# Weighted sums of an attention layer as two float32r matmuls a unit, with the row sums from ones beside v

## The chip, the core and the metric

The kernel runs on one NeuronCore of a Trainium2 chip. The metric is the device time of one execution in microseconds. A core has five engines that work side by side[...]: TensorE (PE in the profile; PEld is its loading of weights), VectorE (DVE), ScalarE (ACT), GpSimd (POOL) and SyncE (SP), which here issues the transfers. Each engine executes its own queue in order.

## What is computed

Two attention layers follow each other on an input of 8 images, 512 channels, 32 x 32 pixels, so T = 1024 positions. Layer 0 is the one that the change touches. Cut to what matters:

```python
# layer 0, per image; 8 heads of 64 channels
h = group_norm(x, gn_w, gn_b)
q, k, v = split(qkv_w @ h + qkv_b)            # per head 64 x T
q, k, v = fake_quant(q), fake_quant(k), fake_quant(v)   # 8 bits, one range over the whole batch
w = softmax((q * scale).T @ (k * scale))      # T x T for each head
a = v @ w.T                                   # 64 x T
x = x + proj_w @ a + proj_b
# layer 1, per image; one head of 512 channels
x = x + wp @ attention(group_norm(x)) + bp
```

The range of fake_quant is that of all images, so no attention of layer 0 can start before the projections of all eight images are done.

## The kernel before

Phase 1 computes q, k and v of all images (`qkps` and `vps`), writes them to device memory and keeps their extremes; then it folds layer 1's weights (`fold`, `fold_b`). Phase 2 does layer 0's attention, its projection (`pj`) and all of layer 1.

The attention of layer 0 runs over units. A unit is one image b, one pair of heads j, one half hf of the 1024 queries and one tile s of 128 keys: 8 x 4 x 2 x 8 = 512 units. The eight units of one (b, j, hf) form a group; there are 64. For each unit `scores` makes two bf16 matmuls of 64 rows, one for each head, into the PSUM tile `st` (128 x 1024, two buffers), and ScalarE takes the exponential into `pt` in SBUF (four buffers). There is no maximum to subtract. VectorE adds the `pt` of a group into `acc`. `weighted` multiplies `pt` by the quantized v in fp32, one 64-column matmul for each head, and accumulates both heads in the two halves of one PSUM bank `av` (two buffers, so that a new group can start while the old bank is read). `finish`, called in the second iteration of the following group, gets the row sums from `acc` with two matmuls by ones (`sm`), copies them to SBUF (`rs`), takes their reciprocal on VectorE and multiplies `av` by it and by the scale of v into `ao`. It also writes one row for each head to `chk0`, from which the end of the kernel decides whether a general path has to redo the work.

The order on TensorE is written out by hand: `mm` ties each matmul to the one before it. `attention` is a generator that issues two units an iteration, in this order:

```python
scores(u + 2)
scores(u + 3)
weighted(u)
weighted(u + 1)
```

The generator `others` issues the projection and layer 1 of the images whose attention is done, in chunks of four fp32 matmuls of 128 x 128 x 512 (`pj`, `g`, `v2ps`, `s`, `o`). A chunk advances a counter by 4.0, an attention iteration advances `pos`, and the loop at the end keeps both in the ratio A_IMAGE / F_IMAGE, so that one image of attention lies beside one image of the other work. Image 0's attention has nothing to lie beside, since the other work needs its result first. In the group norm of layer 1 (`norm_steps`, matmuls `gps`) the other work yields gaps (GN_GAPS 8, 3 and 3), which only attention fills. The tiles of the other work use two PSUM banks (`bank`). Before the loop, `load_pair` fetches q, k and v of the next head pair and quantizes them with two VectorE operations each.

## Time and profile before

| | us |
|---|---|
| median of 3 runs | 3141.29 (3141.09 to 3143.08) |
| the profiled execution | 3143.79 |
| its span | 3142.1 |
| TensorE busy in it | 3058.7 (97%) |
| VectorE busy | 1676.8 (53%) |
| ScalarE busy | 706.2 (22%) |
| first scores of image 0 to its first `pj` | 757.26 to 867.10 |
| start of the last `pj` alone | 2929.53 |

The span is the profiled stretch of one execution. Busy times are of the engines' own instructions; overlapping ones count once in the sum, but their mean length is that of each, so a sum and a mean times a count can differ. A line number is that of the source; L351 is the helper `mm`, so that matmuls there are told apart by their tile names. In a group, the time after the second bar is how long the engine stood idle just before these instructions, and the names after it are what ended that idle time. One fp32 matmul leaves two records. A few per cent of the matmul records can be missing.

### The profile page before, as it was taken

How to read it: one execution, taken by the hardware profiler on the slowest of the kernel's cores; microseconds unless marked ns; L12 is line 12 of the kernel's file. 1: busy time of each engine (PE TensorE's matmuls, PEld its weight loads, DVE VectorE, ACT ScalarE, POOL GpSimd, SP SyncE). 2: the span in 40 equal slices, each digit the busy share in tenths (PEclk: the TensorE clock that was granted, in tenths of full speed). 3: DMA queues.
4: the chain of work that ended last, by engine and by line, in shares of the span. 5: the costliest groups of instructions: out<-in, count | busy, mean ns of one | idle time of the engine just before them, and what ended most of it. 6: DMA issues, size and time to landing. Idle time of an engine off the chain costs nothing.

```text
span 3142.1 us, 22609 instructions
## 1 busy us (share of the span) xinstructions
PE 3058.7 (97%) x8808; PEld 1192.6 (38%) x8808; DVE 1676.8 (53%) x1992; ACT 706.2 (22%) x793; POOL 20.3 (1%) x26
## 2 busy tenths in 40 slices
PE   8999999998899999999999999999999999999998
PEld 4444444444233333333333333333333333333343
DVE  5555544443983555546555645573555546554422
ACT  0000000003632322232223323232322332223001
POOL 0000000000000000000000000000000000000000
PEclk9999999998999999999999999999999999999999
DMA  6222221222110110011010101110110011000000
GB/s 251 101 107 101 100 80 74 80 89 89 61 41 20 47 47 20 23 45 47 21 41 27 61 20 48 43 32 20 48 47 21 27 41 47 21 21 4 14 11 18
DMA packets 90278, 161.55 MB, mean 51 GB/s; under 512 B 11056, under 2 KB 43824, under 8 KB 89520
## 3 DMA queue, kind: packets, MB, share of 16 engines
q1 hardware_dynamic: 88576, 151.32, 13.8%
q10 hardware_dynamic: 1584, 8.68, 0.7%
q8 instruction: 71, 1.16, 0.2%
q14 instruction: 47, 0.39, 0.0%
HBM read 92.56 MB, written 67.11 MB: 51 GB/s over the span
## 4 chain that ended last, share of the span: by engine, by line
PE 90%; DVE 6%; issue 2%; DMA 1%; ACT 0%; POOL 0%; DVEq 0%; ACTq 0%
PE o L351 15%; PE s L351 15%; PE qkps L243 14%; PE av L351 11%; PE g L351 7%; PE v2ps L351 7%; PE vps L262 7%; PE pj L351 7%; PE st L351 3%; DVE acc L407 3%; PE sm L351 2%; DVE rs L429 2%; PE fold L280 1%; PE fold_b L294 1%; DVE acc L405 1%
## 5 line engine op out<-in xcount | busy, mean ns | idle before, releaser
L402 ACT ACTIVATE pt<-st,esc 128x1024 f32<-128x1024 f32 x512 | 544.0, 1112 | 735.8 <-PE st L351 709.1
L351 PE MATMUL av<-pt,v 128*64 128x512 f32 x2048 | 507.6, 617 | 0.0
L407 DVE TENSOR_TENSOR acc<-acc,pt 128x1024 f32<-128x1024 f32 x384 | 467.9, 1220 | 55.0 <-ACT pt L402 43.9
L351 PE MATMUL o<-p,v 128*128 128x512 f32 x1024 | 466.5, 602 | 2.3 <-ACT rs L559 1.4
L351 PE MATMUL s<-g,h 128*128 128x512 f32 x1024 | 465.2, 602 | 0.0
L243 PE MATMUL qkps<-h,wqkv 128*128 128x512 f32 x1024 | 445.4, 596 | 2.6 <-DVE h L115 2.6
L351 PEld LDWEIGHTS o<-p,v 128*128 128x128 f32 x1024 | 186.4, 190 | 275.5 <-issue 233.2
L351 PEld LDWEIGHTS s<-g,h 128*128 128x128 f32 x1024 | 187.1, 190 | 269.7 <-issue 230.0
L243 PEld LDWEIGHTS qkps<-h,wqkv 128*128 128x128 f32 x1024 | 194.3, 191 | 241.7 <-issue 237.2
L429 DVE RECIPROCAL rs<-rs 128x512 f32<-128x512 f32 x64 | 214.6, 3354 | 82.0 <-ACT rs L428 82.0
L351 PE MATMUL g<-h,wa 128*128 128x512 f32 x512 | 236.7, 615 | 6.1 <-DVE h L115 6.1
L351 PE MATMUL pj<-ao,wp 128*128 128x512 f32 x512 | 233.9, 604 | 0.0
L351 PEld LDWEIGHTS av<-pt,v 128*64 128x64 f32 x2048 | 125.7, 137 | 266.0 <-issue 261.1
L351 PE MATMUL v2ps<-wm,h 128*128 128x512 f32 x512 | 222.9, 594 | 0.0
L262 PE MATMUL vps<-wqkv,h 128*128 128x512 f32 x512 | 221.0, 592 | 0.0
L252 DVE TENSOR_SCALAR_CACHE_REDUCE qk<-qkps,qkb 128x1024 f32<-128x1024 f32 x64 | 81.9, 1280 | 195.1 <-PE qkps L243 195.1
L351 PE MATMUL st<-q,k 64*128 64x512 bf16 x1024 | 160.2, 386 | 21.4 <-ACT pt L402 14.4
L526 DVE COPY v<-v2ps 128x512 f32<-128x512 f32 x64 | 44.3, 692 | 256.2 <-PE v2ps L351 256.2
L538 ACT ACTIVATE p<-s 128x512 f32<-128x512 f32 x128 | 76.4, 597 | 433.7 <-PE s L351 433.7
L542 DVE TENSOR_TENSOR acc<-acc,p 128x512 f32<-128x512 f32 x96 | 66.4, 691 | 194.6 <-ACT p L538 194.6
L284 ACT COPY wa<-fold 128x512 f32<-128x512 f32 x4 | 2.3, 585 | 683.5 <-PE fold L280 683.5
L351 PEld LDWEIGHTS g<-h,wa 128*128 128x128 f32 x512 | 97.7, 197 | 146.8 <-issue 114.3
(105 smaller groups left out, 1561.6 us busy)
## 6 DMA issues: line engine op xcount, KB each, us to landing
x<-in_x_dram SPq DMA_DIRECT2D x32, 512.0 KB, 6.3
q_d<-qk SPq DMA_DIRECT2D x32, 512.0 KB, 2.6
k_d<-qk SPq DMA_DIRECT2D x32, 512.0 KB, 2.6
v_d<-v SPq DMA_DIRECT2D x64, 256.0 KB, 2.0
x<-in_x_dram SPq DMA_DIRECT2D x64, 256.0 KB, 2.6
raw<-q_d SPq DMA_DIRECT2D x32, 512.0 KB, 3.4
raw<-k_d SPq DMA_DIRECT2D x32, 512.0 KB, 4.3
raw<-v_d SPq DMA_DIRECT2D x32, 512.0 KB, 4.2
```

What stands on the lines that cost most here:

```text
L243: nc.tensor.matmul(ps[:, hf, :], lhsT=wqkv[:, cc, bass.ts(t, P)], rhs=hn[:, cc, bass.ts(hf, 512)], start=(cc == 0), stop=(cc == CC - 1),)
L252: nc.vector.tensor_scalar(qk, ps.rearrange("p a n -> p (a n)"), qkb[:, t : t + 1], None, ALU.add, ALU.max, accum_out=mx[:, g : g + 1],)
L262: nc.tensor.matmul(ps, lhsT=hn[:, cc, bass.ts(t, P)], rhs=wqkv[:, cc, 2 * C : 3 * C], start=(cc == 0), stop=(cc == CC - 1),)
L280: nc.tensor.matmul(ps, lhsT=wn[lw][:, d, bass.ts(e, P)], rhs=wn[rw][:, d, :], start=(d == 0), stop=(d == CC - 1),)
L294: nc.tensor.matmul(ps[:, oc : oc + 1], lhsT=w[:, e, bass.ts(oc, P)], rhs=vec[:, col + e : col + e + 1], start=(i == 0 and e == 0), stop=(i ...
L351: ins = nc.tensor.matmul(*args, **kw).ins
L402: nc.scalar.activation(pt, st, AF.Exp, scale=esc)
L407: nc.vector.tensor_add(accs[b, j, hf], accs[b, j, hf], pt)
L429: nc.vector.reciprocal(rs, rs)
L526: nc.vector.tensor_copy(vt[:, t, :], ps)
L538: nc.scalar.activation(pt, ps, AF.Exp, scale=SM1)
L542: nc.vector.tensor_add(acc, acc, pt)
```

## The change

The exponential is taken twice for each unit: once into the float32r tile `hi`, which keeps the upper bits, and once in fp32 in place in PSUM. VectorE subtracts the two into a second float32r tile `lo`. Each has three buffers. Both are multiplied by v in float32r, 128 columns at a time: the 128 columns are the 64 of one head's v and 64 of ones, so that each head needs a PSUM bank of its own, and the bank holds the weighted sums in one half and the row sums in the other. A group then takes both banks of `av`. v is kept in two lasting tiles with the ones in the middle. `acc`, its additions and the matmuls `sm` of layer 0 are gone. `finish` is called at the end of the group's own last iteration; it copies the two halves of both banks to SBUF with four ScalarE copies and then works from SBUF. The advances of `pos` and A_IMAGE are new numbers, in about the old ratio. Layer 1's `tt` is gone; that product is written back into its PSUM bank.

```diff
@@ -8,6 +8,7 @@
 from concourse.masks import make_identity
 
 F32 = mybir.dt.float32
+F32R = mybir.dt.float32r
 BF = mybir.dt.bfloat16
 I32 = mybir.dt.int32
 AF = mybir.ActivationFunctionType
@@ -334,7 +335,7 @@
 
         raw_p = fast.enter_context(tc.tile_pool(name="raw", bufs=3))
         qkp = fast.enter_context(tc.tile_pool(name="qkp", bufs=2))
-        ptp = fast.enter_context(tc.tile_pool(name="ptp", bufs=4))
+        ptp = fast.enter_context(tc.tile_pool(name="ptp", bufs=3))
         accp = fast.enter_context(tc.tile_pool(name="accp", bufs=2))
         aop = fast.enter_context(tc.tile_pool(name="aop", bufs=10))
         xp = fast.enter_context(tc.tile_pool(name="xp", bufs=13))
@@ -358,6 +359,12 @@
             nc.vector.tensor_scalar(dst, raw, bhi[:, i : i + 1], MAGIC, ALU.min, ALU.subtract)
 
         HALF = (slice(0, CH), slice(CH, P))
+
+
+        vts = [l1p.tile([P, NT, 3, CH], F32R, name=f"v_{i}") for i in range(2)]
+        for vt in vts:
+            for t in range(NT):
+                nc.scalar.copy(vt[:, t, 1, :], ones[:, 0:CH])
         ao = {}
 
         def load_pair(b, j):
@@ -372,13 +379,16 @@
                 raws.append(raw)
             qt = qkp.tile([P, T], BF, tag="q", name=f"q_{nm}")
             kt = qkp.tile([P, T], BF, tag="k", name=f"k_{nm}")
-            vt = qkp.tile([P, NT, P], F32, tag="v", name=f"v_{nm}")
+            vt = vts[(b * PAIRS + j) % 2]
             quant(raws[0], qt, 0)
             quant(raws[1], kt, 1)
-            quant(raws[2], vt.rearrange("p t d -> p (t d)"), 2)
+            quant(
+                raws[2].rearrange("p (t i d) -> p t i d", t=NT, i=2), vt[:, :, 0:3:2, :], 2
+            )
             return qt, kt, vt
 
         def attention():
+
 
 
 
@@ -386,51 +396,47 @@
             units = [(b, j, hf, s) for b in range(B) for j in range(PAIRS) for hf in range(NH)
                      for s in range(NT)]
             pairs = {(0, 0): load_pair(0, 0)}
-            pts, accs, avs, sums = {}, {}, {}, []
+            pts, avs = {}, {}
 
             def scores(u):
                 b, j, hf, s = units[u]
-                nm = f"{b}_{j}_{hf}"
+                nm = f"{b}_{j}_{hf}_{s}"
                 qt, kt, _ = pairs[b, j]
-                st = pair_ps(f"st_{nm}_{s}")
+                st = pair_ps(f"st_{nm}")
                 for i, r in enumerate(HALF):
                     mm(
                         st[:, i, :], lhsT=kt[r, bass.ts(s, P)],
                         rhs=qt[r, bass.ts(hf, 512)], start=True, stop=True,
                     )
-                pt = ptp.tile([P, 2, 512], F32, tag="p", name=f"pt_{nm}_{s}")
-                nc.scalar.activation(pt, st, AF.Exp, scale=esc)
-                if s == 1:
-                    accs[b, j, hf] = accp.tile([P, 2, 512], F32, tag="acc", name=f"acc_{nm}")
-                    nc.vector.tensor_add(accs[b, j, hf], pts[u - 1], pt)
-                elif s > 1:
-                    nc.vector.tensor_add(accs[b, j, hf], accs[b, j, hf], pt)
-                pts[u] = pt
+                hi = ptp.tile([P, 2, 512], F32R, tag="hi", name=f"hi_{nm}")
+                nc.scalar.activation(hi, st, AF.Exp, scale=esc)
+                nc.scalar.activation(st, st, AF.Exp, scale=esc)
+                lo = ptp.tile([P, 2, 512], F32R, tag="lo", name=f"lo_{nm}")
+                nc.vector.tensor_sub(lo, st, hi)
+                pts[u] = hi, lo
 
             def weighted(u):
                 b, j, hf, s = units[u]
                 if s == 0:
-                    avs[b, j, hf] = av_bank(f"av_{b}_{j}_{hf}")
-                pt = pts.pop(u)
-                for i, r in enumerate(HALF):
-                    mm(
-                        avs[b, j, hf][r, :], lhsT=pairs[b, j][2][:, s, r], rhs=pt[:, i, :],
-                        start=(s == 0), stop=(s == NT - 1),
-                    )
+                    avs[b, j, hf] = [av_bank(f"av_{b}_{j}_{hf}_{i}") for i in range(2)]
+                parts = pts.pop(u)
+                for i, bk in enumerate(avs[b, j, hf]):
+                    w = pairs[b, j][2][:, s, i : i + 2, :].rearrange("p i d -> p (i d)")
+                    for n, part in enumerate(parts):
+                        mm(
+                            bk, lhsT=w, rhs=part[:, i, :],
+                            start=(s == 0 and n == 0), stop=(s == NT - 1 and n == 1),
+                        )
 
             def finish(b, j, hf):
                 nm = f"{b}_{j}_{hf}"
-                acc = accs.pop((b, j, hf))
-                sm = bank(f"sm_{nm}")
-                for i, r in enumerate(HALF):
-                    mm(sm[r, :], lhsT=ones[:, 0:CH], rhs=acc[:, i, :], start=True, stop=True)
                 rs = accp.tile([P, 512], F32, tag="rs", name=f"rs_{nm}")
-                nc.scalar.copy(rs, sm)
+                aot = ao[b, j, hf] = aop.tile([P, 512], F32, tag="ao", name=f"ao_{nm}")
+                for i, bk in enumerate(avs.pop((b, j, hf))):
+                    nc.scalar.copy(rs[HALF[i], :], bk[HALF[1 - i], :])
+                    nc.scalar.copy(aot[HALF[i], :], bk[HALF[i], :])
                 nc.vector.reciprocal(rs, rs)
-                ao[b, j, hf] = aop.tile([P, 512], F32, tag="ao", name=f"ao_{nm}")
-                nc.vector.scalar_tensor_tensor(
-                    ao[b, j, hf], avs.pop((b, j, hf)), scl[:, 2:3], rs, ALU.mult, ALU.mult
-                )
+                nc.vector.scalar_tensor_tensor(aot, aot, scl[:, 2:3], rs, ALU.mult, ALU.mult)
                 row = ((b * PAIRS + j) * NH + hf) * 2
                 for i in range(2):
                     nc.sync.dma_start(
@@ -446,9 +452,6 @@
                     if n < B * PAIRS:
                         pairs[divmod(n, PAIRS)] = load_pair(*divmod(n, PAIRS))
                 yield 0.0, b
-                if s == 2 and u >= NT:
-                    finish(*units[u - NT][:3])
-                    yield 1.0, b
                 if u + 2 < len(units):
 
                     scores(u + 2)
@@ -457,9 +460,10 @@
                     yield 0.25, b
                 weighted(u)
                 weighted(u + 1)
-                yield 2.5, b
-            finish(*units[-1][:3])
-            yield 1.0, B
+                if s == NT - 2:
+                    finish(b, j, hf)
+                yield 2.0, b
+            yield 0.0, B
 
         xts = {}
 
@@ -560,11 +564,10 @@
                         nc.vector.reciprocal(rs, rs)
                         row = b * NH + hf
                         nc.sync.dma_start(chk1[row : row + 1, :], rs[0:1, :])
-                    tt = accp.tile([P, 512], F32, tag="t1", name=f"t1_{b}_{hf}_{dc}")
-                    nc.vector.tensor_mul(tt, ps, rs)
+                    nc.vector.tensor_mul(ps, ps, rs)
                     xx = xt[dc, hf]
                     nc.vector.scalar_tensor_tensor(
-                        xx, tt, ob[:, dc : dc + 1], xx, ALU.add, ALU.add
+                        xx, ps, ob[:, dc : dc + 1], xx, ALU.add, ALU.add
                     )
                     nc.sync.dma_start(out_v[b, :, dc, bass.ts(hf, 512)], xx)
                     yield 4.0
@@ -575,7 +578,7 @@
 
 
         att = attention()
-        A_IMAGE = PAIRS * NH * (NT * 1.5 + 1.0)
+        A_IMAGE = PAIRS * NH * NT * 1.25
         F_IMAGE = 4.0 * (8 + 8 + 8 + 16 + 16)
         pos, done = 0.0, 0
```

## The prediction

> **What bounds the kernel now.** I read the busy shares first, then the costliest groups with their shapes kept apart, then the busy time by stretch, and last the timeline where image 0's attention and a group norm lie.

> ```profile
> PE 3058.7 (97%) x8808; PEld 1192.6 (38%) x8808; DVE 1676.8 (53%) x1992; ACT 706.2 (22%) x793; POOL 20.3 (1%) x26
> ```

> TensorE is busy for nearly the whole span; ScalarE has most of its time free. That average hides two stages. The groups, by shape (operation, operands, count | busy us, mean ns | idle before):

> ```profile
> L402 ACT ACTIVATE pt<-st,esc 128x1024 f32<-128x1024 f32 x512 | 544.0, 1112 | 735.8 <-PE st L351 709.1 <-DVE acc L407 25.7
> L351 PE MATMUL av<-pt,v 128*64 128x512 f32 x2048 | 507.6, 617 | 0.0
> L407 DVE TENSOR_TENSOR acc<-acc,pt 128x1024 f32<-128x1024 f32 x384 | 467.9, 1220 | 55.0 <-ACT pt L402 43.9 <-DVE acc L407 0.5
> L429 DVE RECIPROCAL rs<-rs 128x512 f32<-128x512 f32 x64 | 214.6, 3354 | 82.0 <-ACT rs L428 82.0
> L351 PE MATMUL sm<-acc,ones 128*64 128x512 f32 x256 | 69.0, 617 | 4.0 <-DVE acc L407 3.8
> L428 ACT COPY rs<-sm 128x512 f32<-128x512 f32 x64 | 37.5, 585 | 161.3 <-PE sm L351 161.3
> ```

> The means of `av` and `sm` are of overlapping records: 2048 `av` records of 617 ns fill only 507.6 us, so the two 64-column halves of a unit run beside each other in the array. That decides the gain. Busy time by stretch (length, PE, PEld, DVE, ACT, POOL, granted clock, DMA):

> ```profile
> 757.26:867.10 109.84, 91.31 (x416) 23.52 (x416) 107.96 (x98) 74.55 (x73) 0.00 (x0) 0.97 0.24 74
> 1500.83:1523.09 22.26, 18.53 (x82) 5.16 (x81) 21.73 (x30) 13.20 (x13) 1.01 (x1) 0.87 0.24 72
> 1523.09:1783.00 259.91, 259.77 (x759) 95.76 (x758) 133.07 (x134) 71.31 (x82) 0.00 (x0) 1.00 0.11 35
> ```

> The first is image 0's attention, alone on the core: VectorE is full, 107.96 of 109.84 us. The second is the group norm of image 1, where PE has only attention to run: VectorE full again. The third, the rest of that image: PE has no idle time. There are seven images of the last two kinds (294 us each) and one of the first. In the group norm, PE's timeline shows one iteration (two units):

> ```profile
> 1503.24 0.61 PE L351 MATMUL st<-q,k 64*128 64x512 bf16 x4
> 1503.78 1.94 PE L351 MATMUL av<-pt,v 128*64 128x512 f32 x8
> 1505.65 0.61 PE L351 MATMUL st<-q,k 64*128 64x512 bf16 x4
> ```

> From `st` to the next `st` are 2.41 us: 0.54 for the scores and 1.87 for the weighted sums.

> [...] The trace has 64 fp32 records of `vps` in 27.47 us, 429 ns each, two to a matmul[...]. [...] after an idle time of 2.2 us (861.95 to 864.15) the clock is 0.50 from 866 to 868 us. [...] an fp32 tensor_tensor[...] 691 ns (`acc`, SBUF) and 681 ns (`t`, PSUM operand) for 512.[...]

> **The change, part by part.**

> *Weighted sums, PE.* Per unit there were two fp32 matmuls of 64 columns side by side: four pass times. Now there are two banks times two parts, each one pass over all 128 columns: four pass times. Eight passes an iteration are 8 x 0.2155 = 1.72 us, plus the 0.15 us that the old group also paid at its start (1.87 - 4 x 0.429): 1.87, as before. I count **0**. Float32r is not in the trace: below, 1.72 if the start is hidden (-0.15 x 175 PE-bound iterations = -26 us); above, one record of 429 ns each, 3.58 us with the start (a rival). Weight loads took 190 ns for 128 fp32 columns[...]; if some show, 0.24 us a matmul, +35 us.

> *Row sums, PE.* 64 pairs `sm` go; in PE's timeline one pair, begun at 1496.19, holds PE until the `pj` at 1497.20: 1.01 us. In the seven overlapped images 56 x 1.01 = **-57 us**. In image 0 VectorE sets the pace, so they give nothing there.

> *Exponentials, ACT.* A second Exp per unit, PSUM to PSUM; pairs of L402 take 2.12 us, so 1.06 each: 4.24 us an iteration for 2.12. The trace has no Exp into PSUM; I take the same, from 0.9 to 1.15. *Subtraction, DVE:* 512 of 1.22 us take the place of 448 additions of 1.22. *Finish, ACT:* four copies of 64x512 for one of 128x512; the same 512 columns, so 4 x 0.585 = 2.34 us.

> *What becomes a path.* `pt` had four buffers, and `st` was free as soon as one Exp had read it. Now `st` is held through two Exps and the subtraction, and `hi`, with three buffers, waits for a weighted sum. With PE's order S(u+2) S(u+3) W(u) W(u+1), counted from the end of the second Exp of u+1: subtraction until 1.31 us (0.09 to start, 1.22), S(u+3) until 1.65, the three matmuls that read hi(u) until 2.6; then Exp hi(u+3) and its second, until **4.8**. That is one iteration, for 2.41 (PE) or 3.28 (VectorE: 13.13 us for four, from 809.39 to 822.52) before. All of `load_pair`'s quantizing (0.75 us each) fits in the slack. After a finish, 2.34 us of copies stand ahead of the next Exp, and the reciprocal with its multiply (3.35 + 0.75) ahead of the next subtraction: that one iteration came out at 7.6 us when I followed the three queues by hand, +2.8.

> *Image 0.* Eight groups of 4 x 4.8 + 2.8 = 22.0 us: 176 us. PE then idles some 2.3 us in each iteration, as long as the gap that cost the clock above. At half clock S and W(u) take 1.15 us longer; I charge a third of that, 0.4 x 32 = 13 us. 189 - 110 = **+79 us**.

> *Group norms.* From the end of the last `pj` to the first `g` the instruction order has seven such iterations (six before), two of them with a `gps`. Followed by hand: in the iteration before, `pj` stands between S and W, so hi(u+3) waits for it and S is 2.3 us late; then 4.8, 4.8, 7.6 (finish), 5.1, 6.5 (two `h` operations ahead of a subtraction), 5.6 and the last pair of scores: 39.1 us, and 7 x 0.4 for the clock: 41.9. Before: 22.26, and one iteration of 2.4 more that now lies elsewhere. +17.2 an image, **+120 us** for seven.

> *The rest of an image.* Iterations with two chunks of other work (9.7 us) hide the chain. With one (6.0 us) they just do: 0.53 + 4.24 + 1.3 = 6.05; six an image, 0.3 each with an Exp or copy in the way: **+13 us**. In `S c W` iterations hi(u+3) waits for W behind the chunk, but a chunk follows.

> *At nothing:* filling the ones (16 ACT copies of 64 columns, beside the folds, where ACT waits 675 us); the SP queue, whose DMAs are as many as before, the two `chk` rows of a finish an iteration earlier (1.15 us of issue, nobody waits for them); POOL, whose only work here is the norm's `pow` (1.0 us), moved past nothing; the missing `tt` (multiply into PSUM, 681 ns either way; the bank is held 0.75 us longer, while the next chunk runs 6.9 us); one `av` set in two banks, whose copies are done 6.9 us after the scores, when the next W starts at 9.7; only in the attention-only stretches that is on the path, and counted.

> Sum: +79 + 120 + 13 - 57 + 0 = +155. The profiled execution took 3143.79 us (span 3142.1), 2.5 above the median of 3141.29: 3299, rounded to **3300 us**.

> **The rivals.**

> *A, half clock throughout:* every attention-only iteration takes 5.95. Image 0: 8 x (23.8 + 2.8) = 213, +103; norms 39.1 + 8.1, +22.5 x 7 = 158; +13 - 57: 3358. For it: the gaps of 2.3 us; against: 1.4 us gaps in image 0 left the clock at 1.00.

> *B, only ACT's own work counts:* the queues slide past each other. Image 0: 8 x (17.0 + 2.3) = 154, +44; norms 7 x 4.24 + 2 x 2.34 = 34.4, +9.7 x 7 = 68; -57: 3196. Against: the buffers.

> *C, float32r isn't one pass* (the change not doing what it says): 429 ns each, W 3.58. 175 PE-bound iterations x 1.71 = 299; 81 chain-bound ones x 0.64 (three matmuls) = 52; with the forecast's other terms 3650. For it: every fp32 record here takes 429 ns; against: the change's name for it, which the trace can't test.

> *D, faster:* [...] It decides on the matmul's interval: with the clock held, break-even is near 141 ns.[...]

> **How the numbers follow.** Forecast 0.46, A 0.22, B 0.18, C 0.10, D 0.04. Low 3190 takes in B; high 3440 takes in A and exposed weight loads; C and D are outside. A measurement of this kernel tells some 0.2% (6 us) from no change: faster 0.04, same 0.02, slower 0.94.

> **What would show it.** Right: ACT busy near 1350 us; `hi` waiting on `av`, and `st` on the subtraction; image 0's attention 175 to 215 us; 38 to 48 us from the last `pj` to `g`; `av` at 1.87 us in PE-bound places; no `sm` but layer 1's. Wrong: `av` at 3.4 (C)[...]; image 0 under 160 us (B); idle PE in the g-to-`pj` stretches, which I hold full.

## The result, and the profile after

The changed kernel takes **3248.93 us** (median of four runs, 3243.33 to 3254.29), the kernel before 3142.17 beside it: a ratio of 1.034, 95% interval 1.0321 to 1.0359. The forecast was 3300 in a range of 3190 to 3440, so the side and the range hold and the size was some 50 us too large. The profiled execution took 3250.97 us (span 3249.2); the accounts below are of spans, 107.1 us more than before.

The busy shares of the kernel after, from its profile:

```profile
PE 3060.5 (94%) x8552; PEld 1490.4 (46%) x8552; DVE 1765.1 (54%) x2056; ACT 1333.6 (41%) x1513; POOL 18.1 (1%) x26
```

TensorE's busy time is the same as before to 2 us; the span is 107 longer. So what was lost, on balance, is idle TensorE: 188.7 us of the span for 83.4 before. (The equal sum hides two shifts: TensorE is busy longer in image 0, 121.8 us for 91.3, at a granted clock of 0.75 for 0.97, and shorter beside layer 1.) The groups by shape (operation, operands, count | busy us, mean ns | idle before, what ended it):

```profile
L415 DVE TENSOR_TENSOR lo<-st,hi 128x1024 fp32r<-128x1024 f32 x512 | 623.8, 1219 | 456.0 <-ACT st L413 452.6
L412 ACT ACTIVATE hi<-st,esc 128x1024 fp32r<-128x1024 f32 x512 | 571.4, 1116 | 632.4 <-PE av L352 324.5 <-PE st L352 305.5
L413 ACT ACTIVATE st<-st,esc 128x1024 f32<-128x1024 f32 x512 | 556.5, 1087 | 0.0
L352 PE MATMUL av<-hi,v 128*128 128x512 f32 x1024 | 485.9, 475 | 0.4
L352 PE MATMUL av<-lo,v 128*128 128x512 f32 x1024 | 438.9, 429 | 0.0
L438 DVE RECIPROCAL rs<-rs 128x512 f32<-128x512 f32 x64 | 214.6, 3353 | 37.9 <-ACT rs L436 37.7
L436 ACT COPY rs<-av 64x512 f32<-64x512 f32 x128 | 74.2, 580 | 9.4 <-PE av L352 6.3
L352 PE MATMUL st<-q,k 64*128 64x512 bf16 x1024 | 180.6, 403 | 162.7 <-DVE lo L415 155.2
```

ScalarE's Exp comes twice a unit and waits 324.5 us for `av`, that is for a buffer of `hi`; the scores wait 155.2 us for the subtraction, a wait that the kernel before does not have and that is more than the whole growth of TensorE's idle time (105.3 us). Image 0's attention, a group norm (image 0's) and the rest of the image after it, by their busy times (start and end, length, PE, PEld, DVE, ACT, POOL, granted clock, DMA); the last line is such a rest in the kernel before, also up to the end of its last `pj`:

```profile
760.38:943.60 183.22, 121.76 (x389) 69.99 (x390) 128.47 (x112) 152.32 (x160) 0.00 (x0) 0.75 0.16 49
989.05:1028.53 39.48, 25.48 (x89) 15.45 (x87) 29.81 (x39) 31.16 (x34) 1.06 (x1) 0.82 0.13 41
1028.53:1288.46 259.93, 259.93 (x755) 125.00 (x754) 143.83 (x140) 134.24 (x153) 0.00 (x0) 1.00 0.10 35
...
1523.09:1795.30 272.21, 272.07 (x794) 99.88 (x792) 141.40 (x142) 74.02 (x85) 0.00 (x0) 1.00 0.10 33
```

Image 0's attention and a group norm are longer, and in neither is any engine full: ScalarE has 152 of 183 us, VectorE 128. Before, VectorE was full in both. Where nothing is full, a chain from engine to engine can set the pace. The third stretch, beside layer 1's matmuls, has no idle TensorE at all, and is shorter than before. The timeline of image 0 shows the chain; from the rows of three engines, one turn of it (start, length, engine, instruction, idle time before it and what ended it):

```profile
806.25 1.22 DVE L415 TENSOR_TENSOR lo<-st,hi 128x1024 fp32r<-128x1024 f32 x1 [0.21 <-ACT st L413]
...
807.52 0.39 PE L352 MATMUL st<-q,k 64*128 64x512 bf16 x2 [1.71 <-DVE lo L415]
...
807.84 0.50 PE L352 MATMUL av<-hi,v 128*128 128x512 f32 x1
...
808.90 1.12 ACT L412 ACTIVATE hi<-st,esc 128x1024 fp32r<-128x1024 f32 x1 [0.68 <-PE av L352]
...
809.92 1.08 ACT L413 ACTIVATE st<-st,esc 128x1024 f32<-128x1024 f32 x1
...
811.25 1.22 DVE L415 TENSOR_TENSOR lo<-st,hi 128x1024 fp32r<-128x1024 f32 x1
```

The subtraction ends, frees `st`, and the second score starts (807.52); the weighted sums follow; their first three matmuls free a `hi`, and the Exp starts at 808.90; a second Exp; the next such subtraction starts 5.00 us after the first. From one set of weighted sums to the next, image 0's timeline has 24 turns without a finish. Nine of them take 4.77 to 4.84 us (4.8 was forecast); most of the others take 5.2 to 5.5, and 5.47 is the turn whose weighted sums ran at a granted clock of 0.50.

Where TensorE is the bound, its timeline shows the price of the float32r matmul:

```profile
1384.12 0.50 PE L352 MATMUL av<-hi,v 128*128 128x512 f32 x1
1384.46 0.40 PE L352 MATMUL av<-lo,v 128*128 128x512 f32 x1
1384.70 0.40 PE L352 MATMUL av<-hi,v 128*128 128x512 f32 x1
...
1386.09 7.03 PE L352 MATMUL s<-g,h 128*128 128x512 f32 x16
1393.06 0.61 PE L352 MATMUL st<-q,k 64*128 64x512 bf16 x4
```

After the first, which takes 0.34, the matmuls start 0.23 to 0.24 us apart, one record each, where an fp32 matmul leaves two records 0.43 apart. Eight of them take 1.97 us here and 1.95 at the median, where the old sums took 1.87. The chunk after them takes 6.97 (median 6.96), where one took 7.07 before. So what the sums lose, the next chunk gives back.

### The profile page after: what moved, and what is told of

It reads as the page before. It is cut to its first block, busy times and chain, and to the rows that moved or that the text cites. A ratio compares the mean times of both kernels' runs of the same rounds, so it can differ in the third digit from the quotient of the medians.

```text
span 3249.2 us, 23183 instructions
## 1 busy us (share of the span) xinstructions
PE 3060.5 (94%) x8552; PEld 1490.4 (46%) x8552; DVE 1765.1 (54%) x2056; ACT 1333.6 (41%) x1513; POOL 18.1 (1%) x26
## 4 chain that ended last, share of the span: by engine, by line
PE 88%; ACT 4%; DVE 3%; issue 3%; DMA 1%; POOL 0%; ACTq 0%; DVEq 0%
PE qkps L244 14%; PE o L352 14%; PE s L352 14%; PE av L352 13%; PE g L352 7%; PE pj L352 7%; PE v2ps L352 7%; PE vps L263 7%; PE st L352 4%; DVE lo L415 2%; ACT st L413 2%; ACT hi L412 1%; PE fold L281 1%; PE fold_b L295 1%; PE sm L352 0%
## 5 line engine op out<-in xcount | busy, mean ns | idle before, releaser
L415 DVE TENSOR_TENSOR lo<-st,hi 128x1024 fp32r<-128x1024 f32 x512 | 623.8, 1219 | 456.0 <-ACT st L413 452.6
L412 ACT ACTIVATE hi<-st,esc 128x1024 fp32r<-128x1024 f32 x512 | 571.4, 1116 | 632.4 <-PE av L352 324.5
L413 ACT ACTIVATE st<-st,esc 128x1024 f32<-128x1024 f32 x512 | 556.5, 1087 | 0.0
L352 PE MATMUL av<-hi,v 128*128 128x512 f32 x1024 | 485.9, 475 | 0.4
L352 PE MATMUL o<-p,v 128*128 128x512 f32 x1024 | 455.9, 594 | 1.4 <-ACT rs L563 1.4
L352 PE MATMUL av<-lo,v 128*128 128x512 f32 x1024 | 438.9, 429 | 0.0
L352 PE MATMUL st<-q,k 64*128 64x512 bf16 x1024 | 180.6, 403 | 162.7 <-DVE lo L415 155.2
L352 PEld LDWEIGHTS av<-hi,v 128*128 128x128 f32 x1024 | 213.0, 208 | 128.7 <-issue 77.6
L352 PEld LDWEIGHTS av<-lo,v 128*128 128x128 f32 x1024 | 215.4, 210 | 52.5 <-issue 13.4
L438 DVE RECIPROCAL rs<-rs 128x512 f32<-128x512 f32 x64 | 214.6, 3353 | 37.9 <-ACT rs L436 37.7
L352 PEld LDWEIGHTS <-k 64*128 64x128 bf16 x1024 | 38.9, 95 | 359.8 <-issue 303.0
```

The source lines that it names most:

```text
L352: ins = nc.tensor.matmul(*args, **kw).ins
L412: nc.scalar.activation(hi, st, AF.Exp, scale=esc)
L413: nc.scalar.activation(st, st, AF.Exp, scale=esc)
L415: nc.vector.tensor_sub(lo, st, hi)
L438: nc.vector.reciprocal(rs, rs)
```

## The experiments

Twelve kernels ran. In the table, "image 0" is from its first scores to its first `pj`; "norm" is the mean of the seven stretches from the end of the last `pj` to `g`; "rest" is the time from one `g` to the next without the norm between them (mean of six). In the changed kernel and those made from it, a norm holds about one iteration (2.4 us) that lay in the rest before. All in us; the ratio is to runs of the kernel before made beside each, whose medians were 3139.16 to 3142.80.

| kernel | median | ratio (95%) | image 0 | norm | rest |
|---|---|---|---|---|---|
| before | 3142.17 | 1 | 109.8 | 22.2 | 272.2 |
| after | 3248.93 | 1.034 (1.0321 to 1.0359) | 183.2 | 39.3 | 259.6 |
| e1_hi4 | 3219.85 | 1.0247 (1.023 to 1.0264) | 172.3 | 36.6 | 259.8 |
| e2_early | 3166.99 | 1.0085 (1.0068 to 1.0102) | 157.7 | 31.2 | 259.6 |
| e3_hi_twice | 3037.78 | 0.9676 (0.966 to 0.9692) | 107.8 | 21.3 | 258.6 |
| e4_no_sm | 3077.17 | 0.9803 (0.9787 to 0.982) | 109.0 | 21.9 | 263.4 |
| e5_pool_hi | 3181.71 | 1.0135 (1.0114 to 1.0155) | 167.2 | 32.2 | 259.1 |
| e6_hi_once | 2863.16 | 0.9118 (0.91 to 0.9136) | 101.9 | 20.0 | 235.9 |
| e7_fill | 3250.05 (one run) | | 178.8 | 39.8 | 259.5 |
| e8_pool_hi3 | 3185.34 | 1.0141 (1.0124 to 1.0158) | 163.7 | 33.3 | 259.1 |
| e9_pool_even | 3158.13 | 1.0064 (1.0051 to 1.0078) | 148.2 | 31.3 | 259.5 |
| e10_pool_odd | 3150.16 | 1.0036 (1.0024 to 1.0048) | 153.4 | 30.0 | 258.9 |
| e11_pool_odd_pt3 | 3140.38 | 0.9999 (0.999 to 1.0007) | 145.8 | 29.7 | 259.0 |
| e12_pool_even_pt3 | 3138.54 | 0.9991 (0.9983 to 0.9999) | 144.8 | 29.6 | 259.1 |

The theory was that the chain through `st` and `hi` costs all that is lost, in the stretches with no other work, and that the matmuls themselves gain. The rivals were the clock, and that a shortage of `hi` buffers alone is the cause.

### e3_hi_twice and e4_no_sm: what each half of the change is worth

e3 takes the new chain out and leaves the new matmuls:

```diff
                 nc.scalar.activation(hi, st, AF.Exp, scale=esc)
-                nc.scalar.activation(st, st, AF.Exp, scale=esc)
-                lo = ptp.tile([P, 2, 512], F32R, tag="lo", name=f"lo_{nm}")
-                nc.vector.tensor_sub(lo, st, hi)
+                lo = hi
```

> The changed kernel without the second Exp and without the subtraction; hi is multiplied twice in place of hi and lo, so that TensorE's work and its order are those of the changed kernel (the lower bits are left out and the upper counted twice). Theory (TensorE gains by the change, the chain of Exp and subtraction loses): image 0 about 90 us for 183, group norms about 22 us for 39, the rest as in the changed kernel: 3249 - 93 - 7 x 17 = 3037 us, below the kernel before. Rival (128-column float32r matmuls with 210 ns of weight load each are what costs): not below the kernel before, 3142 us or more.

Measured 3037.78. Image 0 by stretch:

```profile
757.37:865.19 107.82, 96.26 (x388) 54.13 (x389) 51.17 (x46) 88.52 (x94) 0.00 (x0) 0.93 0.25 82
```

107.8 us in place of 183.2. The whole loss lies in the second Exp and the subtraction, with the waits that they bring: 211 us between e3 and the changed kernel, of which 75.4 in image 0, 7 x 18.0 = 126 in the norms and 7 x 1.0 in the rest. What is left of the change, the new matmuls and row sums without VectorE's additions and the smaller parts of the diff with them, is worth a gain of 3.2%. That the total came within 1 us of the 3037 expected is partly luck: image 0 was to fall to 90 us and fell to 107.8 (there `hi` still waits for `av`, 25 times and 12.5 us in all), and norms, rest and first scores made up for it.

e4 takes the two `sm` matmuls out of the kernel before:

```diff
-                sm = bank(f"sm_{nm}")
-                for i, r in enumerate(HALF):
-                    mm(sm[r, :], lhsT=ones[:, 0:CH], rhs=acc[:, i, :], start=True, stop=True)
                 rs = accp.tile([P, 512], F32, tag="rs", name=f"rs_{nm}")
-                nc.scalar.copy(rs, sm)
+                nc.scalar.copy(rs, acc[:, 0, :])
```

> The kernel before without the row-sum matmuls sm of layer 0; rs is copied from acc instead (the sum over partitions is left out). Theory (each pair is worth 1.01 us of TensorE in the seven overlapped images and nothing in image 0): 3142 - 57 = 3085 us. Rival (the order of TensorE has slack, or VectorE's chain to ao takes over): 3142 us.

Measured 3077.17: 63.3 us less than before, some 9 for each of seven images and little in image 0 (0.8). The forecast charged 57: a pair takes 1.01 us, but it also parts two half chunks, which take 3.62 and 3.63 us around it and 7.07 without it.

### e1_hi4: a fourth buffer of hi

```diff
-        ptp1 = fast.enter_context(tc.tile_pool(name="ptp1", bufs=10))
+        ptp1 = fast.enter_context(tc.tile_pool(name="ptp1", bufs=8))
...
-                hi = ptp.tile([P, 2, 512], F32R, tag="hi", name=f"hi_{nm}")
+                hi = ptp.tile([P, 2, 512], F32R, tag="hi", bufs=4, name=f"hi_{nm}")
```

(The tiles `acc1` and `rs1` of layer 1 also get one buffer each, for the room. That costs nothing: the rest, where layer 1 runs, is 259.8 us for 259.6.)

> The changed kernel with a fourth buffer for hi (room made in layer 1: p1 8 buffers for 10, acc1 and rs1 one for two). Theory (the iteration of 4.8 us is set by Exp hi(u+3) waiting for the weighted sum of u, since hi has three buffers): an attention-only iteration falls to ScalarE's own 4.24 us, 0.56 less; image 0 from 183 to about 165 us, a group norm from 39.2 to about 35.3, in all 3249 - 18 - 27 = 3204 us. Rival (st, held through two Exps and the subtraction, sets the pace alone): no change, 3249 us.

Measured 3219.85: 29 us of the 45 expected. The waits of e1 (engine, line, what it waited for: us in all, times, longest):

```profile
ACT hi L412 <- PE st L352: 379.2, 133, 30.0
...
PE st L352 <- DVE lo L415: 143.8, 111, 5.5
```

The wait of `hi` for `av` is gone, but the scores still wait 143.8 us for the subtraction (155.2 after the change). So `hi` was a part of the chain. What is left waits for `st`, which is held through two Exps and a subtraction.

### e2_early: free st after one Exp

(The room for `pt` comes from the same buffers as in e1.)

```diff
-                hi = ptp.tile([P, 2, 512], F32R, tag="hi", name=f"hi_{nm}")
-                nc.scalar.activation(hi, st, AF.Exp, scale=esc)
-                nc.scalar.activation(st, st, AF.Exp, scale=esc)
+                pt = ptp.tile([P, 2, 512], F32, tag="p", bufs=2, name=f"pt_{nm}")
+                nc.scalar.activation(pt, st, AF.Exp, scale=esc)
+                hi = ptp.tile([P, 2, 512], F32R, tag="hi", name=f"hi_{nm}")
+                nc.scalar.copy(hi, pt)
                 lo = ptp.tile([P, 2, 512], F32R, tag="lo", name=f"lo_{nm}")
-                nc.vector.tensor_sub(lo, st, hi)
+                nc.vector.tensor_sub(lo, pt, hi)
```

> The changed kernel with one Exp from PSUM into an fp32 tile in SBUF, from which ScalarE copies hi and VectorE subtracts: the same work on ScalarE and VectorE, but st is free after the first Exp (same room made as in e1; hi and lo keep three buffers). Theory (st held too long is what ties the queues together): W(u) no longer stands behind a late S(u+3), iterations at 4.24 us, and a finish costs only its 2.34 us of copies: image 0 8 x 19.3 = 155 us, group norms 34.4 at the most, in all about 3249 - 28 - 34 = 3187 us. Rival (only the buffers of hi count): between 3204 and 3249 us.

Measured 3166.99: 82 us of the 107 came back, 20 more than expected, by an edit that keeps all the bits and does as many operations. Image 0 by stretch:

```profile
757.96:915.65 157.69, 114.08 (x389) 57.00 (x390) 127.60 (x111) 149.35 (x159) 0.00 (x0) 0.86 0.18 57
```

Now an engine is nearly full: ScalarE 149.35 of 157.69 us, against 152.32 of 183.22. Its work hardly changed; the waits between went.

### e7_fill: is it the clock?

```diff
                     scores(u + 2)
+                    if b == 0:
+                        fill = bank(f"fill_{u}")
+                        for i in range(3):
+                            mm(
+                                fill, lhsT=vts[0][:, 0, 0:2, :].rearrange("p i d -> p (i d)"),
+                                rhs=pts[u][0][:, 0, :], start=True, stop=True,
+                            )
                     yield 0.25, b
```

> The changed kernel with three float32r matmuls of no use between the two scores of each of image 0's iterations, where TensorE waits 2.3 us, so that its clock is not taken down. Theory (the half clock lengthens image 0's iterations, 183 us for 176 at full clock): clock in image 0 near 1.00 for 0.75, its attention about 176 us, in all 3242 us. Rival (the chain of Exp and subtraction hides the clock): 183 us as before, or longer.

Image 0 by stretch:

```profile
757.53:936.32 178.79, 130.71 (x484) 76.29 (x485) 127.83 (x112) 151.37 (x159) 0.00 (x0) 0.91 0.16 50
```

The granted clock rose from 0.75 to 0.91, and image 0 became 4.4 us shorter. Of the 24 turns without a finish, 16 now take 4.78 to 4.79 us, for nine near that before, and eight still 5.1 to 5.5; those with a finish take 6.8 to 7.1 (6.3 to 7.0 before), and the extra matmuls stand in the queue too. What the 24 turns take above 4.79 each is 9.7 us in the changed kernel and 4.6 here. So the low clock costs some 10 of the 73 us in image 0, an estimate from these turns; as the cause of the loss the rival falls. The whole, in one run, is no shorter than without the filling.

### e5_pool_hi and e8_pool_hi3: the copy on GpSimd

e2 with one line changed, to unload ScalarE:

```diff
-                nc.scalar.copy(hi, pt)
+                nc.gpsimd.tensor_copy(hi, pt)
```

> As e2_early, with the copy that makes hi moved from ScalarE to GpSimd, which is idle in this stage. Theory (in e2 ScalarE's own 4.24 us an iteration is what is left; taken off it, TensorE and VectorE set the pace): if GpSimd takes 2 us or less for 128x1024, image 0 about 125 us for 158, group norms about 25 us for 31, in all 3167 - 33 - 7 x 6 = 3092 us, below the kernel before. Rival (GpSimd's copy is longer than ScalarE's two operations, 2.1 us a unit): it becomes the bound, and at 4 us a copy image 0 takes 260 us and the kernel over 3250.

Measured 3181.71, 15 us *slower* than e2: neither the gain nor the rival's price. Image 0 of e5 by stretch:

```profile
757.36:924.52 167.16, 122.88 (x389) 60.16 (x390) 143.34 (x110) 89.01 (x94) 89.49 (x65) 0.81 0.17 53
```

ScalarE fell from 149 to 89 us as meant, but VectorE rose from 127.60 to 143.34 with the same operations. Two pairs of rows of e5's timeline show why (start, length):

```profile
835.85 1.04 POOL L414 CAST hi<-pt 128x1024 fp32r<-128x1024 f32 x1 [0.40 <-ACT pt L412]
835.92 2.05 DVE L416 TENSOR_TENSOR lo<-pt,hi 128x1024 fp32r<-128x1024 f32 x1
...
838.56 1.21 DVE L416 TENSOR_TENSOR lo<-pt,hi 128x1024 fp32r<-128x1024 f32 x1
839.24 1.43 POOL L414 CAST hi<-pt 128x1024 fp32r<-128x1024 f32 x1 [2.35 <-ACT pt L412]
```

The cast that starts first takes 1.04 us, and the subtraction that starts 0.07 later takes 2.05 in place of 1.22; in the second pair the subtraction is first and keeps its 1.21, and the cast takes 1.43. No idle time stands before the longer subtraction: the 0.83 us show only in the length of the instruction. From 780 us to the end of image 0, reciprocals apart, 35 VectorE operations that a cast joined later were not lengthened (-0.01 to +0.01 us), while 21 that began during a cast were, by 0.15 us where 0.35 of the cast were left, up to 0.84 where 0.97 were. Three reciprocals that began with 0.98 us of a cast left kept their 3.34 us. So the delay is the cast's rest less 0.13 to 0.2 us. What the two engines have in common there is not shown.

e8 is e5 with a third buffer for `pt`, from one `ao` and one `x` (the edit against e2):

```diff
-                pt = ptp.tile([P, 2, 512], F32, tag="p", bufs=2, name=f"pt_{nm}")
+                pt = ptp.tile([P, 2, 512], F32, tag="p", name=f"pt_{nm}")
...
-                nc.scalar.copy(hi, pt)
+                nc.gpsimd.tensor_copy(hi, pt)
```

> As e5_pool_hi, with a third buffer for the fp32 tile pt (room: ao 9 buffers for 10, x 12 for 13). Theory (in e5 the two buffers of pt tie Exp, GpSimd's copy and the subtraction into one chain of 1.06 + 1.2 to 1.8 + 1.23 us for each buffer, and ScalarE waits 162 us for the subtraction): the queues come apart, VectorE is left as the bound of an attention-only iteration with some 3.3 to 4 us; image 0 about 140 us for 167, group norms about 26 us for 31, in all 3182 - 27 - 35 = 3120 us, below the kernel before by 0.7%. Rival (GpSimd's copy and VectorE slow each other down in SBUF, and that is what e5 paid): no change from e5, 3182 us.

Measured 3185.34: the rival. Image 0 of e8 by stretch:

```profile
757.40:921.07 163.67, 117.28 (x388) 59.34 (x389) 154.43 (x108) 87.97 (x95) 87.28 (x66) 0.81 0.16 51
```

The group of its subtraction, over the whole run:

```profile
L416 DVE TENSOR_TENSOR lo<-pt,hi 128x1024 fp32r<-128x1024 f32 x512 | 743.4, 1480 | 301.5 <-POOL hi L414 300.5
```

With the buffer more VectorE operations begin during a cast (50 in the whole of image 0, reciprocals included, for 32 in e5): the mean subtraction goes 1220 (e2), 1453 (e5), 1480 ns (e8), and VectorE is busy 154.43 of 163.67 us.

### e9 to e12: half the copies on GpSimd

The cure for an exclusion is to meet it less. e9 and e10 divide e2's copies (the comment is added here):

```diff
-                nc.scalar.copy(hi, pt)
+                if s % 2 == 0:      # e9; in e10: == 1
+                    nc.gpsimd.tensor_copy(hi, pt)
+                else:
+                    nc.scalar.copy(hi, pt)
```

> All bits kept. e2_early, with the copy into hi on GpSimd for the first unit of each iteration and on ScalarE for the second. In the trace of e5_pool_hi a GpSimd cast and a VectorE operation exclude each other: the one that starts first keeps its time (35 VectorE operations beside a cast that began later: 0.00 us longer), the other is longer by about what is left of the first (0.83 us where 0.97 us of a cast were left). If that is the whole cost, half the casts cost half of e5's extra VectorE time. An iteration then asks 3.2 us of ScalarE (two Exps and one copy, for 4.2 in e2) and some 2.7 of VectorE; with the finish a group takes about 18 us: image 0 about 146 us (e2: 157.7), a group norm about 28.5 (31.1), the whole 3137 us (3125 to 3155). Rival: any use of GpSimd costs about what all of it does, through its start after the semaphore (0.4 us) and not through the exclusion; then the time lies between e2 and e5, about 3175 us.

> All bits kept. As e9_pool_even, but the second unit's copy on GpSimd and the first's on ScalarE. ScalarE's order is then Exp, copy, Exp, and the cast of the second unit starts 3.2 us into the iteration, while VectorE still subtracts for the first unit (2.1 to 3.4) or quantizes. If the exclusion is what costs, this order meets it more often than e9's, where the cast of the first unit ends before VectorE has its first subtraction: mean subtraction 1.25 us or below in e9, 1.30 or above here, and the time 5 to 15 us above e9's. Rival: the order makes no difference, within 4 us.

Measured 3158.13 and 3150.16, both below e2. Half the casts did free most of the VectorE time: the mean subtraction is 1216 ns in e9, and 1230 in e10 where 1300 or more was expected, as in e2 (1220). But e9 is above its range, and the order of the two is the reverse of what the expectation said. e10's image 0 is 5 us longer, but its norms are 2.0 shorter (28.9 against 30.9 in six of the seven), seven times over. Nor did e10 meet the exclusion more often: 12 VectorE operations of its image 0 began during a cast, four of them in its last 0.11 us, and 15 of e9's. Two differences lie in those norms. In e9 ScalarE's copy waits 2.5 us a norm for a weighted sum, where in e10 such waits fall on GpSimd, which has time; and e9's quantizing of k and v, which begins during a cast, is 1.1 us longer. Which of them makes the 2.0 us is not shown; e12 below keeps the wait, and its norms are as short as e11's.

e11 and e12 are e10 and e9 with e8's third buffer of `pt`.

> All bits kept. e10_pool_odd with a third buffer of pt; its room comes from one of the ten ao and one of the thirteen x buffers. In image 0 of e10 ScalarE waited 25.1 us for a subtraction to free pt (27 times). If that wait sets the pace there, most of it comes back in image 0 (153.4 us to about 135) and some 2 us in each group norm (28.9 to about 27): 3120 us, below the kernel before. Rival: VectorE is the pace already (two subtractions, a fourth of the finish's 4.1 us and the quantizing make 3.75 us an iteration, 120 us in image 0, before any wait for GpSimd), more casts then lie beside its work, and the wait only changes its name, as from e5 to e8: within 5 us of e10's 3150.

> All bits kept. e9_pool_even with a third buffer of pt, room as in e11. ScalarE's two Exps of an iteration then no longer wait for the subtraction two units back, and the cast of the first unit moves ahead, away from VectorE's quantizing (15 VectorE operations of e9's image 0 waited for a cast, 0.79 us each at most). If the buffer is the pace: image 0 148.2 to about 138, norms 30.9 to about 28, 3128 us. Rival, VectorE is the pace: within 5 us of e9's 3158.

Measured 3140.38 and 3138.54, between the two theories: 10 and 20 us below e10 and e9, but not the 30 that a freed ScalarE was to bring. e11's image 0 by stretch has VectorE nearly full again, with 135.15 of 145.81 us:

```profile
757.29:903.10 145.81, 109.96 (x388) 54.52 (x389) 135.15 (x110) 118.64 (x128) 43.27 (x33) 0.87 0.20 61
```

Both keep all the bits and are level with the kernel before (intervals 0.999 to 1.0007 and 0.9983 to 0.9999). They gain 13 an image in the rest, and lose 35 to 36 in image 0 and 7.5 in each norm.

### e6_hi_once: one part

```diff
-                nc.scalar.activation(st, st, AF.Exp, scale=esc)
-                lo = ptp.tile([P, 2, 512], F32R, tag="lo", name=f"lo_{nm}")
-                nc.vector.tensor_sub(lo, st, hi)
-                pts[u] = hi, lo
+                pts[u] = (hi,)
```

(The flag that ends an accumulation moves to the one part that is left.)

> The changed kernel with hi alone, multiplied once (the lower bits of the exponentials are left out): no second Exp, no subtraction, half the weighted-sum matmuls. Theory (a one-pass matmul costs 0.23 us of TensorE in the PE-bound places): 4 x 0.23 = 0.93 us an iteration less than e3_hi_twice, 175 of them, -163 us; image 0 and the group norms, bound by ScalarE there, some 8 and 2 us each shorter: 3038 - 163 - 22 = about 2853 us. Rival (the others' queues become the bound once TensorE has less to do): 2950 us or more.

Measured 2863.16, 8.8% below the kernel before: with half the weighted-sum matmuls and no chain both stages gain (rest 235.9 for 259.6, norm 20.0). It is the fastest of all, at the price of the lower bits. e3 and e4 are below the kernel before too, but e3 counts the upper bits twice and e4 leaves out the sum over partitions.

## Why the prediction was right in kind and 50 us too high

| term | forecast | measured |
|---|---|---|
| image 0 | +79 | 183.2 - 109.8 = +73 |
| group norms (less the iteration moved in, 2.4 each) | +120 | 7 x (39.3 - 22.2 - 2.4) = +103 |
| iterations beside one chunk | +13 | 7 x 1.0 = +7 |
| row sums | -57 | -62 to -63 (e4) |
| weighted sums and chunks | 0 | 7 x (-2.4) = -17 |
| later first scores | 0 | +3 |
| sum | +155 | +107 |

*The chain: right.* Its turn of 4.8 us was measured at 4.79 at full clock, `hi` waits on `av` and `st` on the subtraction as said, and ScalarE is busy 1333.6 us (1350 said). e3 shows that the chain is all of the loss, e1 and e2 that both of the named buffers, `hi` and `st`, make it.

*Group norms: the mis-sized term.* The turns that were followed by hand come to 39.1 us, and 39.3 is the measured mean; that the two agree is partly luck. The clock's losses, charged as 2.8 on top, are there (turns of 5.3 to 5.5 for 4.8 and 5.1 in the norm that starts at 989.05, granted clock 0.82). But over the seven norms the turn with the finish takes 6.9 on average for 7.6, and the last one with its pair of scores 5.5 for some 6.1, while the two forecast at 4.8 take 5.05 and 5.6. So the charge for the clock was offset by a finish and an end that were priced too high. This is 17 of the 48 us between forecast and measurement.

*Image 0.* The finish again: the turn with it was forecast at 7.6 and came at 6.3 to 7.0, over seven turns 6.3 us less in all. The clock was charged with 13 us and its turns show 9.7.

*Row sums.* The 1.01 us of a pair was right; the chunks that it parts, which e4 shows, were not counted.

*Weighted sums.* Forecast at 1.87 us, they take 1.95. That a float32r matmul is one pass, 0.2155 us or about half of an fp32 record of 429 ns, was the author's estimate, which no trace of the kernel before could show; with new weights at each it took 0.23 us. That alone would be +14 us, inside the bounds given. But 2.4 us an image came back: I compare e3's rest (258.6) with before's less the moved iteration and e4's saving (272.2 - 2.4 - 8.8 = 261.0). The first weights of a chunk behind weighted sums were loaded only when it began; now they are loaded under the last of the sums, and the chunk takes 0.10 less. From the timelines of weight loads (PEld) and matmuls, before and after:

```profile
1605.92 0.30 PEld L351 LDWEIGHTS s<-g,h 128*128 128x128 f32 x2 [0.81 <-ACT pt L402]
1605.92 3.70 PE L351 MATMUL s<-g,h 128*128 128x512 f32 x8
...
1385.86 0.43 PEld L352 LDWEIGHTS s<-g,h 128*128 128x128 f32 x2
1386.09 7.03 PE L352 MATMUL s<-g,h 128*128 128x512 f32 x16
```

In the 18 iterations of an image where scores stand just ahead of the weighted sums, 0.08 is lost and 0.10 gained. In the other seven a half chunk (once layer 1's `sm`) stands between, and there the first weights of the sums are loaded early too: half chunk and weighted sums take 5.38 us (from 1409.06 to 1414.44) for 5.50 before (from 1621.83 to 1627.33), and the chunk behind another 0.10 less. Together that is some -0.4 and -1.6 of the -2.4 us an image; for the last 0.4 I have no line.

*One-chunk iterations.* Half of what was said: the rest differs by 1.0 us from e3's, which has no chain.

*Later first scores.* The first scores start at 760.38 for 757.26. e12, which fills the same ones, starts at 760.51, and the other runs with the same filling at 757.3 to 758.0: it is no cost of the change.

*The rivals.* A (half clock throughout) gave 213 us for image 0, for 183.2 measured, and falls with e7. C (429 ns a matmul) and D (141 ns or less) fall by the measured 0.23 us. B, in which only ScalarE's own work counts, gave 154 us for image 0 and 34.4 for a norm; that is not the changed kernel, but nearly e2 (157.7 and 31.2), where the buffers no longer hold it back. The argument against B, "the buffers", was the right one.

*Slips in the working.* 0.53 + 4.24 + 1.3 is 6.07 and not 6.05; the rivals' totals start from the median and the forecast's from the profiled execution, 2.5 us above it; and the norm at 1500.83 is that of image 2, counted from 0, not of image 1. None of them moves the forecast by more than 2.5 us.

## What to carry to other kernels

An exact split into two cheaper operands moves work from TensorE to the engines that feed it: count what the split holds (PSUM tile, buffer) and for how long, in the stretches where nothing else covers it, before counting what the matmuls gain. Copy the source out and free the PSUM tile after one read, then split from SBUF; that alone gave back 82 of 107 us. Work moved to a second engine can lengthen the instructions of one that is nearly full, here the mean subtraction from 1220 to 1453 ns with all copies on GpSimd, and cost more than it takes over; and a part of the work moved can be worth more than all of it: all copies on GpSimd took 15 us more than none, and half of them 9 to 17 us less.
